# Context projections of layers 1 to 3 beside the first steps of layer 0's recurrence

## The chip, the cores and the metric

The kernel runs on one core of one Trainium2 chip. The metric is the device time of one execution in microseconds (us). The engines are named as in the profile: PE is TensorE (PEld its weight loads), DVE is VectorE, ACT is ScalarE, POOL is GpSimd, SP is SyncE, whose queue (SPq) issues most DMAs. L12 is line 12 of the kernel before, unless the text says that it is the changed kernel's.

## The reference, cut to what matters

Four layers work on tokens x (4 batches of 512 tokens, width 256) and a context (4 batches of 64 rows, width 256). Each layer adds an attention over the context and a feed-forward part, each behind a layer norm and a gate.

```python
# layer 0: an LSTM over the 512 tokens, attending to the context in each step;
# then one of 8 experts per token
x = x + tanh(g_xattn[0]) * _L0_xattn_ref(ctx_1024, _layernorm(x), ...)
x = x + tanh(g_ffn[0]) * _L0_ffn_ref(_layernorm(x), ...)
# layer 1: attention in both directions; two of 8 experts
x = x + tanh(g_xattn[1]) * _L1_xattn_ref(_layernorm(x), ctx_1024, ...)
    K_sub = _linear(subword_emb, Wk_s, bk_s)     # of the context alone
    V_sub = _linear(subword_emb, Wv_s, bv_s)
    Q_sub = _linear(subword_emb, Wq_s, bq_s)
...
# layer 2: additive attention; the experts that hold 0.8 of the probability
    txt_proj = einsum('btd,de->bte', textual_features, Ws)   # context alone
# layer 3: 16 heads of 64; then an int8 matmul
    k = (context @ Wk.T).reshape(b, nk, H, DH)   # context alone
    v = (context @ Wv.T).reshape(b, nk, H, DH)
```

The six lines marked or named by the context (K_sub, V_sub, Q_sub, txt_proj, k, v) need nothing of x. All arithmetic is float32 but for the last matmul.

## The kernel before, in words

**Setup** (lstm, L245). SP loads the LSTM's weights, then the first two pairs of expert weights (two calls of fetch, four DMAs of 1 MB) into a ring of three slots, each with a place for an up and a down matrix, 1 MB each. The transposed context, ctxT, stays for the whole kernel.

**Recurrence** (L360). The 512 steps of layer 0 are a serial chain, one lstm_step each: h times two weights on PE (L816, L825), the attention's tanh on ACT (L834), scores on PE (L843), softmax, attended features into the gates (L867), transpose of the gates (L875, DVE), gate arithmetic, and the new h (hb, L893, DVE). Each instruction of a step is pinned to the program's order on its engine. Work that is not on the chain is put in a planner, Later (L162): tasks with an engine, a cost, and the tasks that they wait for. At fixed places of each step, fill emits as many as fit a budget: on PE one after whh's matmuls, two after the scores and two after the gates' (SLOT_A, SLOT_B, SLOT_C), on DVE one between alb (L863) and the transpose of the gates (L875). A task goes out only when what it needs on another engine was emitted one step earlier for DVE and ACT, four for SP. Before step 64 the planner holds the projections of the gates for later tokens (every 32 steps); after each block of 64 steps (TB), block_tasks adds the experts of layer 0 for that block. The planner's accumulators "up" have two buffers. An expert matrix is fetched (L111, the DMAs are L122 and L125) when the last matmul of the one before in its place is done. After the last step the planner is drained.

Instructions that are not pinned are placed by a scheduler: if an instruction's tile is free early in the program, it may land among the recurrence's.

**Tail.** Layer 1 starts with norm (xn, L988) and its loads (load_l1, L1497: wqc, wks, wvs, wqs, wkc, wvc, wg, b, interp, in this order on SP). context_l1 (L1515) first makes hbg from b, then 4 projections for ksT and qsT (two matmuls each, 128x256) and 4 for vs. load_l2 (L1649) and context_l2 (L1665) do the same for layer 2: wslide from its vector l_vec (L1672), txtT (two projections), rep (L1682), and off from the mask (L1690 to L1692). All matmuls of the tail stand in program order on PE, and are listed under the helper's line L936.

The experts of layers 1 and 2 are run in two halves of two batches each: b0 and b1 (layer 1), c0 and c1 (layer 2). weave (L906) takes one piece of the main generator, an expert's pieces, and then side pieces at a given ratio; part_of ends the side part after a number of pieces. back (L1461) is such a side part: it gathers expert rows for 128 tokens with an indirect DMA issued by POOL (yg, L1477, 8 buffers) and adds each to the tokens on DVE (L1469), the add standing more than three pairs behind. Beside c1 run the backs of batches 0 and 1 and the start of layer 3: load_l3 (L1782: wk, wv, wq, wo, bo, rhs), context_l3 (L1800: kT, 8 projections evicted by DVE, L1812; v, 4 of width 512 evicted by ACT), then heads and the int8 matmul. The backs of batches 2 and 3 follow c1.

Of the kernel before, what the change touches and what calls it, by code (L numbers as in the profile page):

```python
# [21 lines left out]
FP = mybir.dt.float32  # L22
# [222 lines left out]
def lstm(net):  # L245
    tc, nc, a = net.tc, net.nc, net.a
    with ExitStack() as st:
# [19 lines left out]
        with tc.tile_pool(name="l_set", bufs=1) as pool, tc.tile_pool(  # L267
# [21 lines left out]
            nc.sync.dma_start(w1b, a["L0_whh1"])  # L289
            net.fetch()  # L290
            net.fetch()

# [68 lines left out]
def recurrence(net, w, pools):  # L361
# [21 lines left out]
    h = w["h0"]  # L383
    for t in range(S):
        i, u = divmod(t, P)
        if u == 0 and i + 1 < TPB:
            norm_x(net, later, w, pools, xb, i + 1)
        v = t % TB
        if v == 0:
            n = t // TB  # L390

            assert n < 3 or all(x["at"] for x in used[n - 3])
            hb = two.tile([P, 2, TB, NB], FP, name="hb", bufs=3)
            cb = two.tile([P, 2, TB, NB], FP, name="cb", bufs=3)
        if t % 32 == 0 and t and t // 32 + 1 < NJ:
            gates_of_block(net, later, w, pools, xb, ge, t // 32 + 1)
        lstm_step(net, pools["step"], ps, w, later, ge, t, h, hb[:, :, v], cb[:, :, v], ga[t % 2], ga[1 - t % 2])
        h = hb[:, :, v]
        if t > TB and t % 8 == 4:
            net.fill()  # L400
        if v == TB - 1:
            used.append(block_tasks(net, later, w, moe0, pools, n, hb, cb))
    later.drain()


# [1055 lines left out]
def back(t, pool, kind, batches, group, got):  # L1461
# [9 lines left out]
    for b in batches:  # L1471
        for i in range(TPB):
            for k in range(0, kind.most, 2):
                here = []
                for kk in (k, k + 1):
                    y = pool.tile([P, D], FP, name="yg", bufs=8)
                    nc.gpsimd.indirect_dma_start(  # L1477
                        out=y[:, :], out_offset=None, in_=got["res"][:, :],
                        in_offset=bass.IndirectOffsetOnAxis(
                            ap=got["index"][:, b - group[0], kk, i : i + 1], axis=0  # L1480
                        ),
                    )
                    c = got["cw"][:, b - group[0], kk, i : i + 1]
                    here.append((y, net.xtok[:, b * TPB + i, :], c))
                due.append(here)
                if len(due) > 3:
                    add()
                yield
# [8 lines left out]
def load_l1(net, pool):  # L1497
    nc, a = net.nc, net.a
    w = {}
    for n in ("wqc", "wks", "wvs", "wqs", "wkc", "wvc"):  # L1500
        w[n] = pool.tile([P, KD, D], FP, name=f"l1_{n}")
        nc.sync.dma_start(w[n], a[f"L1_{n}"])
    w["wg"] = pool.tile([P, 2 * KD, D], FP, name="l1_wg")
    nc.sync.dma_start(w["wg"], a["L1_wg"])
    w["b"] = pool.tile([P, 7, 2], FP, name="l1_b")
    nc.sync.dma_start(w["b"], a["L1_b"])
    w["interp"] = pool.tile([SC, S], FP, name="l1_interp")
# [6 lines left out]

def context_l1(t, w, pool):  # L1515

    net = t.net
    nc = t.nc

    w["hbg"] = pool.tile([P, 2], FP, name="hbg")  # L1520
    nc.vector.tensor_scalar_mul(w["hbg"], w["b"][:, 6, :], 0.5)
    for n in ("ks", "qs"):
        w[f"{n}T"] = pool.tile([P, 2, NB * SC], FP, name=f"{n}T")
        for oc in range(2):
            ps = t.ps(P, NB * SC)
            mm(nc, ps, ((w[f"w{n}"][:, k, ts(oc, P)], net.ctxT[:, k, :]) for k in range(KD)))
            nc.vector.tensor_scalar_add(w[f"{n}T"][:, oc, :], ps, w["b"][:, BIAS[n], oc : oc + 1])
    w["vs"] = pool.tile([SC, NB, D], FP, name="vs")
    for b in range(NB):
        ps = t.ps(SC, D)  # L1530
        mm(nc, ps, ((net.ctxT[:, k, ts(b, SC)], w["wvs"][:, k, :]) for k in range(KD)))
        nc.vector.tensor_copy(w["vs"][:, b, :], ps)

# [115 lines left out]
def load_l2(net, pool):  # L1649
    nc, a = net.nc, net.a  # L1650
    w = {}
    for n in ("ws", "w"):
        w[n] = pool.tile([P, KD, D], FP, name=f"l2_{n}", tag="rt" if n == "ws" else "l2_w")
        nc.sync.dma_start(w[n], a[f"L2_{n}"])
    w["vec"] = pool.tile([P, 4, KD], FP, name="l2_vec")
    nc.sync.dma_start(w["vec"], a["L2_vec"])
    w["bc"] = pool.tile([P, 2], FP, name="l2_bc")
# [6 lines left out]

def context_l2(t, w, pool):  # L1665

    net = t.net
# [4 lines left out]
    nc.vector.tensor_copy(w["wslide"][:, :, 31], w["vec"][:, 0, :])  # L1672
    w["txtT"] = pool.tile([P, KD, NB * SC], FP, name="txtT")
    for ec in range(KD):
        ps = t.ps(P, NB * SC)
        mm(nc, ps, ((w["ws"][:, k, ts(ec, P)], net.ctxT[:, k, :]) for k in range(KD)))
        nc.vector.tensor_scalar_add(w["txtT"][:, ec, :], ps, w["vec"][:, 1, ec : ec + 1])
        yield
    w["cw"] = pool.tile([P, 2, NB * SC], FP, name="cw")
# [102 lines left out]
def load_l3(net, pool):  # L1782
    nc, a = net.nc, net.a
    w = {}
    w["wq"] = pool.tile([P, KD, 1024], FP, name="l3_wq")

    wkv = pool.tile([P, 2, KD, 1024], FP, name="l3_wkv", tag="atT")
    w["wk"], w["wv"] = wkv[:, 0], wkv[:, 1]
    for n in ("wk", "wv", "wq"):
        nc.sync.dma_start(w[n], a[f"L3_{n}"])  # L1790
    w["wo"] = pool.tile([P, NP, D], FP, name="l3_wo")
# [7 lines left out]

def context_l3(t, w, pool):  # L1800

# [3 lines left out]
    nc.vector.memset(w["ones"], 1.0)  # L1805
    w["kT"] = pool.tile([P, NP, NB * SC], FP, name="kT")

    w["v"] = pool.tile([P, NB, NP, 64], FP, name="v")
    for pr in range(NP):
        ps = t.ps(P, NB * SC)  # L1810
        mm(nc, ps, ((w["wk"][:, k, ts(pr, P)], net.ctxT[:, k, :]) for k in range(KD)))
        nc.vector.tensor_copy(w["kT"][:, pr, :], ps)  # L1812
        yield
    for b in range(NB):
        ps = t.ps(P, 512)
        for par in range(2):
            mm(nc, ps[ts(par, 64), :], (
                (net.ctxT[:, k, ts(b, SC)], w["wv"][:, k, ts(par, 512)]) for k in range(KD)
            ))
        nc.scalar.copy(w["v"][:, b].rearrange("p n d -> p (n d)"), ps)  # L1820
        yield

# [169 lines left out]
def gated_blocks_kernel(ctx: ExitStack, tc: tile.TileContext, a, out):  # L1992
# [5 lines left out]
    for layer, kind in KINDS.items():  # L1998
        for g, x in enumerate(got[layer]):
            x["rows"] = net.scratch(f"rows{layer}{g}", kind.rows, kind.end)  # L2000
            x["res"] = net.scratch(f"res{layer}{g}", kind.end, kind.end)
    lstm(net)
    t = Tail(net, ctx)
# [3 lines left out]
    t.b1 = mp.tile([P, 3, F_MOE[2] // P], FP, name="b1_in")  # L2007
    with ExitStack() as right, ExitStack() as work:

# [7 lines left out]
        with tc.tile_pool(name="attn1", bufs=1) as p1:  # L2017
            w1 = load_l1(net, p1)
            w2 = load_l2(net, p2)
            context_l1(t, w1, p1)  # L2020
            pk = Picks(t, sort)
# [19 lines left out]
            run(behind(1, l1, 0))  # L2041
            weave(b0.sure(), chain(behind(1, l1, 2), context_l2(t, w2, p2)), 1.1)
            b0.rest()
# [15 lines left out]
    def layer3(b, over=False):  # L2059
        return chain(heads(t, w3, p3, b, over), quantised(t, w3, p3, b, out))  # L2060

    start = chain(
        back_of(2, 0, [0]), turns(context_l3(t, w3, p3), back_of(2, 0, [1])), layer3(0), layer3(1)
    )
    weave(c1.sure(), part_of(start, 105), 0.8)
    c1.rest()
# [116 lines left out]
```

## Time and profile before

| what | value |
|---|---|
| median of three timed runs | 5496.51 us (5494.62 to 5498.4) |
| profiled execution | 5493.01 us, of which its span is 5491.3 |
| mean granted PE clock | 0.954 |
| PE busy | 4605.5 us (84%) |
| DVE busy | 2441.6 us (44%) |
| ACT busy | 2532.1 us (46%) |
| POOL busy | 466.3 us (8%) |
| recurrence, first to last h | 54.26 to 3463.69 us |

The page of the profile lists busy times, the span in 40 slices, DMA queues, the chain that ended last, and the costliest groups of instructions. The timeline of an engine has one row per instruction or run of equal instructions: start, duration, engine, line, operation, tiles and shapes, and in brackets how long the engine stood idle before and what ended that. The windows give the engines' busy times and the granted clock of a stretch. A float32 matmul appears as two passes, so two matmuls are four rows of PE.

### The profile page before, as it was taken

How to read it: one execution, taken by the hardware profiler on the slowest of the kernel's cores; microseconds unless marked ns; L12 is line 12 of the kernel's file. 1: busy time of each engine (PE TensorE's matmuls, PEld its weight loads, DVE VectorE, ACT ScalarE, POOL GpSimd, SP SyncE). 2: the span in 40 equal slices, each digit the busy share in tenths (PEclk: the TensorE clock that was granted, in tenths of full speed). 3: DMA queues.
4: the chain of work that ended last, by engine and by line, in shares of the span. 5: the costliest groups of instructions: out<-in, count | busy, mean ns of one | idle time of the engine just before them, and what ended most of it. 6: DMA issues, size and time to landing. Idle time of an engine off the chain costs nothing. (4 is left out here: it accounts for less than half of the span.)

```text
span 5491.3 us, 139195 instructions
## 1 busy us (share of the span) xinstructions
PE 4605.5 (84%) x57504; PEld 2504.8 (46%) x57504; DVE 2441.6 (44%) x9780; ACT 2532.1 (46%) x7118; POOL 466.3 (8%) x884
## 2 busy tenths in 40 slices
PE   5566699789999899999999989987978598869967
PEld 2222244334444344444444434754533365757744
DVE  3545555555555555555555555224422342121145
ACT  2233365556656566566556555412266265213212
POOL 1000100000100100000000000001111201230030
PEclk8999999999999999999999999988999799989978
DMA  5000022122212122122122111313543333543210
GB/s 191 2 2 2 2 78 109 40 74 94 93 67 102 54 90 94 61 75 97 68 81 102 71 42 49 118 40 130 194 140 126 136 117 120 191 158 136 94 53 8
DMA packets 117963, 480.46 MB, mean 87 GB/s; under 512 B 23473, under 2 KB 62786, under 8 KB 87938
## 3 DMA queue, kind: packets, MB, share of 16 engines
q1 hardware_dynamic: 105026, 437.85, 22.3%
q0 software_dynamic: 12288, 33.57, 1.9%
q8 instruction: 455, 7.45, 0.6%
q14 instruction: 194, 1.59, 0.1%
HBM read 434.65 MB, written 137.89 MB: 104 GB/s over the span
## 5 line engine op out<-in xcount | busy, mean ns | idle before, releaser
L867 PE MATMUL psf<-fw,alb 128*4 128x256 f32 x8192 | 540.7, 381 | 171.4 <-DVE alb L863 141.0
L720 PE MATMUL ps_up<-xm,ring 128*128 128x256 f32 x2048 | 614.8, 412 | 3.4 <-ACT h L730 3.3
L751 PE MATMUL ps_down<-ring,h 128*128 128x256 f32 x2048 | 580.5, 399 | 0.0
L825 PE MATMUL psf<-whh,hb 128*4 128x256 f32 x8176 | 542.4, 383 | 0.0
L720 PEld LDWEIGHTS ps_up<-xm,ring 128*128 128x128 f32 x2048 | 335.9, 188 | 226.7 <-issue 174.2
L855 ACT ACTIVATE al<-psr,stat 128x64 f32<-128x64 f32 x1024 | 312.4, 309 | 272.6 <-DVE stat L854 272.0
L751 PEld LDWEIGHTS ps_down<-ring,h 128*128 128x128 f32 x2048 | 356.9, 189 | 156.9 <-issue 111.6
L834 ACT ACTIVATE e<-e 128x256 f32<-128x256 f32 x512 | 213.4, 417 | 466.4 <-DVE e L833 465.3
L854 DVE TENSOR_REDUCE stat<-psr 128x1 f32<-128x64 f32 x1024 | 229.5, 225 | 419.7 <-PE psr L843 409.2
L833 DVE TENSOR_TENSOR e<-fproj,hw 128x256 f32<-128x256 f32 x1024 | 395.4, 427 | 17.6
L816 PE MATMUL psa<-wh,hb 128*4 128x64 f32 x8176 | 209.7, 220 | 228.1 <-DVE hb L893 226.6
L843 PE MATMUL psr<-e,vrep 128*32 128x64 f32 x16384 | 349.8, 224 | 47.1 <-ACT e L834 41.8
L474 PE MATMUL psf<-ge,ident 128*4 128x256 f32 x4096 | 319.7, 384 | 65.2 <-DVE gt L875 65.1
L894 POOL COPY cb<-ga 128x8 f32<-128x8 f32 x512 | 97.0, 189 | 3234.2 <-DVE ga L886 3234.2
L843 PEld LDWEIGHTS psr<-e,vrep 128*32 128x32 f32 x16384 | 262.5, 109 | 236.2 <-ACT e L834 228.4
L936 PE MATMUL ps_up<-xT,ring 128*128 128x256 f32 x1280 | 309.5, 393 | 72.2 <-ACT h L1425 52.3
L1717 ACT ACTIVATE h<-featT,txtT 128x512 f32<-128x512 f32 x512 | 324.7, 710 | 97.5 <-PE psr L936 64.1
L878 ACT ACTIVATE ga<-gt 128x32 f32<-128x32 f32 x512 | 116.8, 228 | 541.9 <-DVE gt L875 541.7
L875 DVE STREAM_TRANSPOSE gt<-psf 128x256 f32<-128x256 f32 x512 | 230.3, 450 | 302.7 <-PE psf L867 302.2
L867 PEld LDWEIGHTS psf<-fw,alb 128*4 128x4 f32 x8192 | 117.0, 84 | 518.2 <-DVE alb L863 517.7
L816 PEld LDWEIGHTS psa<-wh,hb 128*4 128x4 f32 x8176 | 114.5, 86 | 487.2 <-DVE hb L893 487.2
L936 PEld LDWEIGHTS ps_up<-xT,ring 128*128 128x128 f32 x1280 | 244.4, 195 | 150.0 <-ACT h L1425 55.7
(418 smaller groups left out, 6565.7 us busy)
## 6 DMA issues: line engine op xcount, KB each, us to landing
ring<-in_L_w_dram SPq DMA_DIRECT2D x208, 1024.0 KB
ring<-in_L_w_dram SPq DMA_DIRECT2D x120, 512.0 KB
res<-y SPq DMA_DIRECT2D x120, 128.0 KB
rows_in<-rows SPq DMA_DIRECT2D x40, 256.0 KB
rows_in<-rows SPq DMA_DIRECT2D x40, 128.0 KB
rows<-in_x_dram SPq DMA_DIRECT2D x2, 1920.0 KB
res<-in_x_dram SPq DMA_DIRECT2D x2, 1920.0 KB
xtok<-in_x_dram SPq DMA_DIRECT2D x4, 512.0 KB
```

What stands on the lines that cost most here:

```text
L474: net.tc.keep_in_program_order(net.nc.tensor.matmul(out[32 * q : 32 * q + NB, :], lhsT=sel, rhs=ge[t // 32][:, ts(q, 256)], start=True, st ...
L720: yield nc.tensor.matmul(cell["ps"][:, f % 2, :], lhsT=ex["w"][:, k, ts(f, P)], rhs=box["x"][:, k, :], start=k == 0, stop=k == KD - 1,)
L751: yield nc.tensor.matmul(cell["ps"], lhsT=ex["h"][:, f, ts(p, P)], rhs=ex["down"][:, f, :], start=f == 0, stop=f == 7,)
L816: pin(nc.tensor.matmul(ps["a"][32 * q : 32 * q + NB, :], lhsT=h[:, c, :], rhs=w["wh"][:, c, ts(q, 64)], start=c == 0, stop=c == 1,))
L825: pin(nc.tensor.matmul(psf[32 * q : 32 * q + NB, :], lhsT=h[:, c, :], rhs=w["whh"][:, c, ts(q, 256)], start=False, stop=False,))
L833: pin(nc.vector.tensor_add(e[:, p], w["fproj"][:, p], bc(hw[:, :, ts(p, 2)], 3, SC)))
L843: pin(nc.tensor.matmul(ps["r"][p][ts(2 * b + i, 32), :], lhsT=w["vrep"][:, c, :], rhs=ev[:, ::-1, :] if i else ev, start=c == 0, stop=c == ...
L855: pin(nc.scalar.activation(al[:, p], ps["r"][p], AF.Exp, bias=stat[:, p, 0:1], accum_out=stat[:, p, 1:2]))
L867: pin(nc.tensor.matmul(psf[32 * q : 32 * q + NB, :], lhsT=alb[:, p], rhs=w["fw"][:, p, ts(q, 256)], start=False, stop=p == 1,))
L875: pin(nc.vector.transpose(gt.rearrange("p g b -> p (g b)"), psf))
L936: return lambda *a, **k: self.tc.keep_in_program_order(fn(*a, **k))
L1717: nc.scalar.activation(h, featT[:, ec, :], AF.Tanh, bias=w["txtT"][:, ec, col : col + 1])
```

## The change

The projections that need only the context and weights move to the start of the kernel. load_context loads their weights and the vectors of layers 1 and 2 in the setup, where the experts' first fetches stood; the four small matrices share one place of the ring, wk and wv take one place each. context_tasks gives the planner 26 jobs at step 4, one accumulator each: 4 for ksT and qsT, 4 for vs, 2 for txtT, 8 for kT (two matmuls each) and 8 for v (four matmuls each, of width 256 in place of 512); all are evicted by DVE. The experts' four fetches are emitted at step 60. The results lie in new pools on the right side of the memory, allocated ahead of the recurrence (16 KB per partition for kT and v, some 10 KB for the rest), and the pools that were on the right start behind them. The gathers' buffers go from 8 to 6, the adds stand more than two pairs behind, and the side pieces beside c1 go from 105 to 93, at a ratio of 0.7 for 0.8. What is left of context_l1, context_l2 and context_l3 is renamed.

```diff
--- before.py
+++ after.py
@@ -287,8 +287,7 @@
             nc.sync.dma_start(small[:, 28:36], a["L0_bhh1"])
             nc.sync.dma_start(w1, a["L0_wih1"])
             nc.sync.dma_start(w1b, a["L0_whh1"])
-            net.fetch()
-            net.fetch()
+            load_context(net)
@@ -382,6 +381,12 @@
     gates_of_x(net, ps["f"], ge, 0)
     h = w["h0"]
     for t in range(S):
+        if t == 4:
+            context_tasks(net, later, pools["up"])
+        if t == TB - 4:
+            assert not later.left()
+            net.fetch()
+            net.fetch()
@@ -401,6 +406,84 @@
     later.drain()
+
+
+def load_context(net):
+
+    nc, a, c = net.nc, net.a, net.of_context
+    r = net.ring
+    for i, n in enumerate(("L1_wks", "L1_wqs", "L1_wvs", "L2_ws")):
+        c[n] = r[:, 0, 0, ts(i, 512)].rearrange("p (k d) -> p k d", k=KD)
+    for i, n in enumerate(("L3_wk", "L3_wv")):
+        c[n] = r[:, i, 1 - i].rearrange("p (k d) -> p k d", k=KD)
+    nc.sync.dma_start(c["b"], a["L1_b"])
+    nc.sync.dma_start(c["vec"], a["L2_vec"])
+    for n in ("L1_wks", "L1_wqs", "L1_wvs", "L2_ws", "L3_wk", "L3_wv"):
+        nc.sync.dma_start(c[n], a[n])
+
+
+def context_tasks(net, later, up):
+
+    nc, c, ctxT = net.nc, net.of_context, net.ctxT
+    v = nc.vector
+
+    def job(shape, parts, out, cost=1.0, after=()):
+        box, head = {}, None
+        for of, lhsT, rhs, k in parts:
+
+            def part(of=of, lhsT=lhsT, rhs=rhs, k=k):
+                if not box:
+                    box["ps"] = up.tile(shape, FP, name="ps_cx", tag="up")
+                yield nc.tensor.matmul(
+                    of(box["ps"]), lhsT=lhsT, rhs=rhs, start=k == 0, stop=k == KD - 1
+                )
+
+            last = later.add("PE", part, after, cost, takes=[] if head else ["up"])
+            head = head or last
+        later.add("DVE", lambda: [out(box["ps"])], [last], frees=[("up", head)])
+
+    def all_of(x):
+        return x
+
+    n = NB * SC
+    for name in ("ks", "qs"):
+        for oc in range(2):
+            job(
+                [P, n], [(all_of, c[f"L1_w{name}"][:, k, ts(oc, P)], ctxT[:, k, :], k) for k in range(KD)],
+                lambda ps, name=name, oc=oc: v.tensor_scalar_add(
+                    c[f"{name}T"][:, oc, :], ps, c["b"][:, BIAS[name], oc : oc + 1]
+                ),
+            )
+    for b in range(NB):
+        job(
+            [SC, D], [(all_of, ctxT[:, k, ts(b, SC)], c["L1_wvs"][:, k, :], k) for k in range(KD)],
+            lambda ps, b=b: v.tensor_copy(c["vs"][:, b, :], ps),
+        )
+    for ec in range(KD):
+        job(
+            [P, n], [(all_of, c["L2_ws"][:, k, ts(ec, P)], ctxT[:, k, :], k) for k in range(KD)],
+            lambda ps, ec=ec: v.tensor_scalar_add(c["txtT"][:, ec, :], ps, c["vec"][:, 1, ec : ec + 1]),
+        )
+    for pr in range(NP):
+        job(
+            [P, n], [(all_of, c["L3_wk"][:, k, ts(pr, P)], ctxT[:, k, :], k) for k in range(KD)],
+            lambda ps, pr=pr: v.tensor_copy(c["kT"][:, pr, :], ps),
+        )
+
+    for b in range(NB):
+        for h in range(2):
+            job(
+                [P, 256], [
+                    (
+                        lambda ps, par=par: ps[ts(par, 64), :], ctxT[:, k, ts(b, SC)],
+                        c["L3_wv"][:, k, ds(512 * par + 256 * h, 256)], k,
+                    )
+                    for par in range(2) for k in range(KD)
+                ],
+                lambda ps, b=b, h=h: v.tensor_copy(
+                    c["v"][:, b, ts(h, 4)].rearrange("p n d -> p (n d)"), ps
+                ),
+            )
@@ -1473,7 +1556,7 @@
             for k in range(0, kind.most, 2):
                 here = []
                 for kk in (k, k + 1):
-                    y = pool.tile([P, D], FP, name="yg", bufs=8)
+                    y = pool.tile([P, D], FP, name="yg", bufs=6)
@@ -1483,7 +1566,7 @@
...
                 due.append(here)
-                if len(due) > 3:
+                if len(due) > 2:
@@ -1497,13 +1580,13 @@
 def load_l1(net, pool):
     nc, a = net.nc, net.a
     w = {}
-    for n in ("wqc", "wks", "wvs", "wqs", "wkc", "wvc"):
+    for n in ("wqc", "wkc", "wvc"):
         w[n] = pool.tile([P, KD, D], FP, name=f"l1_{n}")
         nc.sync.dma_start(w[n], a[f"L1_{n}"])
     w["wg"] = pool.tile([P, 2 * KD, D], FP, name="l1_wg")
     nc.sync.dma_start(w["wg"], a["L1_wg"])
-    w["b"] = pool.tile([P, 7, 2], FP, name="l1_b")
-    nc.sync.dma_start(w["b"], a["L1_b"])
+    for n in ("b", "ksT", "qsT", "vs"):
+        w[n] = net.of_context[n]
@@ -1512,24 +1595,10 @@
 BIAS = {n: i for i, n in enumerate(("qc", "ks", "vs", "qs", "kc", "vc", "g"))}
 
 
-def context_l1(t, w, pool):
-
-    net = t.net
-    nc = t.nc
+def gate_bias(t, w, pool):
 
     w["hbg"] = pool.tile([P, 2], FP, name="hbg")
-    nc.vector.tensor_scalar_mul(w["hbg"], w["b"][:, 6, :], 0.5)
...
+    t.nc.vector.tensor_scalar_mul(w["hbg"], w["b"][:, 6, :], 0.5)
@@ -1649,11 +1718,10 @@
 def load_l2(net, pool):
     nc, a = net.nc, net.a
     w = {}
-    for n in ("ws", "w"):
-        w[n] = pool.tile([P, KD, D], FP, name=f"l2_{n}", tag="rt" if n == "ws" else "l2_w")
-        nc.sync.dma_start(w[n], a[f"L2_{n}"])
-    w["vec"] = pool.tile([P, 4, KD], FP, name="l2_vec")
-    nc.sync.dma_start(w["vec"], a["L2_vec"])
+    w["w"] = pool.tile([P, KD, D], FP, name="l2_w")
+    nc.sync.dma_start(w["w"], a["L2_w"])
+    for n in ("vec", "txtT"):
+        w[n] = net.of_context[n]
@@ -1662,20 +1730,13 @@
-def context_l2(t, w, pool):
-
+def constants_l2(t, w, pool):
     net = t.net
     nc = t.nc
 
     w["wslide"] = pool.tile([P, KD, 63], FP, name="wslide")
     nc.vector.memset(w["wslide"], 0.0)
     nc.vector.tensor_copy(w["wslide"][:, :, 31], w["vec"][:, 0, :])
...
@@ -1783,11 +1844,9 @@
     nc, a = net.nc, net.a
     w = {}
     w["wq"] = pool.tile([P, KD, 1024], FP, name="l3_wq")
-
-    wkv = pool.tile([P, 2, KD, 1024], FP, name="l3_wkv", tag="atT")
-    w["wk"], w["wv"] = wkv[:, 0], wkv[:, 1]
-    for n in ("wk", "wv", "wq"):
-        nc.sync.dma_start(w[n], a[f"L3_{n}"])
+    nc.sync.dma_start(w["wq"], a["L3_wq"])
+    for n in ("kT", "v"):
+        w[n] = net.of_context[n]
@@ -1797,28 +1856,12 @@
-def context_l3(t, w, pool):
+def constants_l3(t, w, pool):
 
     net = t.net
     nc = t.nc
     w["ones"] = pool.tile([1, P], FP, name="ones")
     nc.vector.memset(w["ones"], 1.0)
...
@@ -1999,13 +2042,24 @@
+
+    late = ctx.enter_context(tc.tile_pool(name="late", bufs=1, side="right"))
+    right = ExitStack()
+    early = right.enter_context(tc.tile_pool(name="early", bufs=1, side="right"))
+    net.of_context = {
+        name: pool.tile(shape, FP, name=f"cx_{name}") for name, pool, shape in (
+            ("b", early, [P, 7, 2]), ("vec", early, [P, 4, KD]), ("ksT", early, [P, 2, NB * SC]),
+            ("qsT", early, [P, 2, NB * SC]), ("vs", early, [SC, NB, D]),
+            ("txtT", early, [P, KD, NB * SC]), ("kT", late, [P, NP, NB * SC]), ("v", late, [P, NB, NP, 64]),
+        )
+    }
     lstm(net)
...
-    with ExitStack() as right, ExitStack() as work:
+    with right, ExitStack() as work:
@@ -2017,7 +2071,7 @@
         with tc.tile_pool(name="attn1", bufs=1) as p1:
             w1 = load_l1(net, p1)
             w2 = load_l2(net, p2)
-            context_l1(t, w1, p1)
+            gate_bias(t, w1, p1)
@@ -2039,7 +2093,7 @@
             b1 = Blocks(t, KINDS[1], first, got[1][1], KINDS[1].sure % 3)
             b0 = Blocks(t, KINDS[1], first, got[1][0], 0, b1)
             run(behind(1, l1, 0))
-            weave(b0.sure(), chain(behind(1, l1, 2), context_l2(t, w2, p2)), 1.1)
+            weave(b0.sure(), chain(behind(1, l1, 2), constants_l2(t, w2, p2)), 1.1)
@@ -2060,9 +2114,9 @@
     start = chain(
-        back_of(2, 0, [0]), turns(context_l3(t, w3, p3), back_of(2, 0, [1])), layer3(0), layer3(1)
+        back_of(2, 0, [0]), turns(constants_l3(t, w3, p3), back_of(2, 0, [1])), layer3(0), layer3(1)
     )
-    weave(c1.sure(), part_of(start, 105), 0.8)
+    weave(c1.sure(), part_of(start, 93), 0.7)
```

More of the change, by code (lines that the diff above doesn't have):

```diff
@@ L1512 @@
 BIAS = {n: i for i, n in enumerate(("qc", "ks", "vs", "qs", "kc", "vc", "g"))}
-def context_l1(t, w, pool):
-    net = t.net
-    nc = t.nc
+def gate_bias(t, w, pool):
     w["hbg"] = pool.tile([P, 2], FP, name="hbg")
[L1521 to L1532, printed above, removed]
+    t.nc.vector.tensor_scalar_mul(w["hbg"], w["b"][:, 6, :], 0.5)
 def both_ways(t, w, pool, b):
@@ L1672, in context_l2 @@
     nc.vector.tensor_copy(w["wslide"][:, :, 31], w["vec"][:, 0, :])
[L1673 to L1678, printed above, removed]
     w["cw"] = pool.tile([P, 2, NB * SC], FP, name="cw")
@@ L1805, in context_l3 @@
     nc.vector.memset(w["ones"], 1.0)
[L1806 to L1821, printed above, removed]
     w["identb"] = pool.tile([P, P], BF, name="identb")
```

## Prediction

> **What bounds the kernel now.** I read the page's forty slices first, then the DVE and SP timelines of the first slices, then the windows of the stages that the change touches, then the PE groups and the POOL timeline of the last layers.
>
> ```profile
> PE   5566699789999899999999989987978598869967
> PEclk8999999999999999999999999988999799989978
> ```
>
> A slice is 137 us. Slices 0 to 24 are the recurrence of layer 0, a serial chain of 512 steps; the rest are experts' matmuls, with dips of PE and of its clock where layers meet. No one engine bounds the whole, so each moved piece must be priced in its own stage.
>
> The update of h (DVE, L893) ends each step. Between steps 5 and 40 it comes every 6.50 us. In steps 2 to 4 it does not:
>
> ```profile
> 60.48 0.17 DVE L893 SCALAR_TENSOR_TENSOR hb<-ga,tcn 128x8 f32<-128x8 f32 x1 [0.28 <-ACT tcn L888]
> 79.87 0.17 DVE L1672 COPY wslide<-l_vec 128x2 f32<-128x2 f32 x1 [15.48 <-DMA l_vec<-in_L_vec_dram]
> 83.85 0.17 DVE L893 SCALAR_TENSOR_TENSOR hb<-ga,tcn 128x8 f32<-128x8 f32 x1 [0.34 <-ACT tcn L888]
> 92.54 0.17 DVE L893 SCALAR_TENSOR_TENSOR hb<-ga,tcn 128x8 f32<-128x8 f32 x1 [0.33 <-ACT tcn L888]
> 100.38 0.17 DVE L893 SCALAR_TENSOR_TENSOR hb<-ga,tcn 128x8 f32<-128x8 f32 x1 [0.33 <-ACT tcn L888]
> ```
>
> The differences are 23.37, 8.69 and 7.84. DVE stands 15.48 us before a constant of layer 2 that the scheduler put among step 2's instructions, since its tile was free from the start. Its DMA is late because SP was held:
>
> ```profile
> 43.91 17.05 SPq L513 DMA_DIRECT2D xh<-in_x_dram  x4
> 74.46 0.33 SPq L1656 DMA_DIRECT2D l_vec<-in_L_vec_dram  x1
> ```
>
> The three other stages, from the windows (columns: stretch, its length, busy time and count of each engine, granted clock, DMA share, GB/s):
>
> ```profile
> core 0: us, PE busy (x) PEld busy (x) DVE busy (x) ACT busy (x) POOL busy (x), PEclk, DMA share, GB/s
> 54.00:101.00 47.00, 22.49 (x382) 8.46 (x382) 14.45 (x67) 8.85 (x40) 5.64 (x9) 0.65 0.52 174
> 3627.00:3648.00 21.00, 14.19 (x45) 9.27 (x46) 4.99 (x14) 0.40 (x1) 0.00 (x0) 0.62 0.33 107
> 4900.00:4960.00 60.00, 60.00 (x282) 47.26 (x281) 5.31 (x10) 16.36 (x39) 0.00 (x0) 1.00 0.44 152
> ```
>
> The second is layer 1's start, a chain on a slow clock. The third is a stretch of layer 2's second half (c1) in which PE is full: work taken from PE there comes off the end.
>
> **The change part by part**, against the profiled execution, 5493.0 us (span 5491.3 and 1.7 around it). The median of the three timed runs is 3.5 us above it; I add that at the end.
>
> *Early steps.* In the changed program's order, layer 2's DVE constants stand behind the last step: the new pools on the right push layer 2's pool onto memory that the recurrence uses. The layer's vector is loaded with the first transfers, and no other DVE instruction of the early steps waits for a DMA. So the excess goes: 16.9 + 2.2 + 1.3 = **-20.4**. Next late is the step's own chain, 6.50.
>
> *The added jobs.* From step 4, one per step: 26 jobs, 68 matmuls and 26 evictions. An eviction (0.42 us for a copy, 0.48 with a bias, by the rows of kT and ksT) stands on DVE ahead of this row, whose idle covers it:
>
> ```profile
> 59.08 0.45 DVE L875 STREAM_TRANSPOSE gt<-psf 128x256 f32<-128x256 f32 x1 [0.74 <-PE psf L867]
> ```
>
> Behind it on DVE is the gate chain of the step. Two matmuls (four 128x256 passes at 0.216 us) go into a step, four for a v job. Later steps that already carry expert matmuls show 6.58 against 6.50, so 26 x 0.08 = **+2.1**. From both sides: 0, and 0.28 per step (the 6.78 of steps with gates' work), +7.3. SP issues nine transfers at the start instead of four, five more at 0.45, 2.3 us; behind them are tables and rows that only the first experts' tasks need, after step 64, which hide it. The experts' four fetches move to step 60 and wait there for the jobs' matmuls, which ended by step 30; one is hoisted to the start. 4 MB at 174 GB/s is 24 us, under the four steps (26 us) to the first possible use; without that cover, up to 24.
>
> *Layer 1's start.*
>
> ```profile
> 3624.41 1.38 DVE L988 TENSOR_SCALAR xn<-xtok,ln_mv,ln_rstd 128x256 f32<-128x256 f32 x4
> 3636.52 0.17 DVE L1521 TENSOR_SCALAR hbg<-l_b 128x2 f32<-128x2 f32 x1 [10.72 <-DMA l_wg<-in_L_wg_dram]
> ```
>
> ```profile
> 3630.40 3.75 PE L936 MATMUL ps_side<-ctxT,l_wks 128*128 128x256 f32 x8 [6.63 <-DMA l_wks<-in_L_wks_dram]
> 3637.12 3.78 PE L936 MATMUL ps_side<-ctxT,l_wqs 128*128 128x256 f32 x8 [2.98 <-DVE ksT L1527]
> 3645.56 0.49 PE L936 MATMUL ps_side<-upper,ones 128*128 128x128 f32 x2
> 3647.87 2.41 PE L936 MATMUL ps_side<-xT,l_wqc 128*128 128x512 f32 x5 [0.34 <-DVE xT L1003]
> ```
>
> The normalised tokens are ready at 3625.8, the projections of the context stand in front, and wqc's matmuls start at 3647.87. Without them wqc decides, issued at 3626.99; wks landed 3.0 us after its issue, so about 3630.4: -17.5. But the clock: wks' passes run at half speed for some 10 us, and now the token projections meet that. From both sides 0 and 5 us (half of 10); I take 3, since steady matmuls replace a broken chain: **-14.5** (-12.5 to -17.5). The Trainium skill's page "TensorE: Matmul & The Clock Gate", Part 1, has the clock doubled after about 3.4 us of sustained matmuls; by that the loss is half of 3.4, an estimate of 1.7, and the sum would be 1.3 lower. The trace's slow passes last longer, with waits between them, so it does not decide that.
>
> *Layer 2's start.* Two txtT jobs leave a PE-bound stage: 8 passes of 0.216, **-1.7** (0 to -2.7).
>
> *c1.*
>
> ```profile
> L936 PE MATMUL ps_side<-ctxT,l_wkv 128*128 128x256 f32 x32 | 8.2, 379 | 0.0
> L936 PE MATMUL ps_side<-l_wkv,ctxT 128*64 128x512 f32 x32 | 7.8, 605 | 0.0
> ```
>
> The 32 passes for kT start 0.216 apart: 6.9. The v passes start in pairs 14 ns apart, each job from 4934.51 to 4936.38, with 0.2 lost at its ends: four jobs, 8.2. **-15.1** (0 to -16).
>
> *Fewer gather buffers.* Issue to the end of the add is 3.2 to 7.3 us where DVE is prompt; six buffers at 1.25 us each cover 7.5. Where DVE is held, POOL stops two gathers sooner, as it already does here:
>
> ```profile
> 5261.16 0.95 POOL L1477 DMA_INDIRECT yg<-res,g_index  x1 [4.26 <-DVE xtok L1469]
> ```
>
> Two gathers are 2.5 us, and the tail's 48 gathers lie on the chain that ends last: **+2.5** (0 to +8, three such stops). Behind the stopped gather on POOL are only gathers; the adds wait for them. The page "DMA: Bandwidth & Descriptors" of the Trainium skill, "Anatomy of one DMA", gives about 2.0 us plus the bytes for a GpSimd DMA; by it (2.3 us, an estimate) six buffers would never be short and the term 0. The 3.2 to 7.3 here are longer.
>
> *Moved constants.* Four DMAs of layer 2 now stand on SP after the last step, ahead of a ring fetch (4 x 0.4 us); the mask's conversion then holds DVE some 3 us with an add of experts' output behind it, where DVE shows 2 to 13 us idle before each add and PE has its next expert: 0 to +3. The sorter's constants and the gate bias go to layer 1's start. Together **+1**.
>
> Sum: -20.4 + 2.1 - 14.5 - 1.7 - 15.1 + 2.5 + 1 = -46.1; 5493.0 becomes 5446.9, on the median's scale **5450.4**.
>
> **Rivals**, on that scale.
> *The early stall finds another cause* (a job's matmul waits in PE's queue for its weights). For: SP's 17 us hold stays. Against: those weights are issued before it, where ring fetches stood. 5450 + 20 = 5471.
> *c1 does not shorten*, since transfers or the gathers set its end. For: PE idles 39.76 us there. Against: 60.00 of 60 and 0.44 DMA share. 5466.
> *Slower: the gathers collide with more expert transfers.* In before, one store of expert rows sat behind three 1 MB fetches while 48 gathers shared the DMA engines, and PE stood:
>
> ```profile
> 4868.91 3.48 PE L936 MATMUL ps_up<-xT,ring 128*128 128x256 f32 x8 [39.76 <-ACT h L1425]
> ```
>
> With 0.7 side pieces per expert piece and no kT and v between, the second batch's gathers fall beside other fetches. Each repeat costs 39.8; the gain of 46 is gone, and 11 more, from 57 us of new PE idle, so two repeats: 5530. Against: the tail's 48 gathers show none.
> *The collision falls away instead*: 5411.
> *The jobs hide nothing*: 18 jobs' 72 passes and 32 paired v passes at half speed (0.43) are 45, evictions 12, in all 57 instead of 2.1: 5505. Against: the 6.58 row.
>
> **How the numbers follow.** A measurement here tells about 0.2% (11 us) from no change. Forecast (5436 to 5464) 0.56; early stall 0.12; c1 0.13; collisions 0.06; collision gone 0.08; jobs on the path 0.05. The first three hold 0.81, and with their bounds reach 5430 to 5480. Faster 0.89, same 0.05, slower 0.06.
>
> **What would show it.** h every 6.5 to 6.8 us from step 2; no DVE wait for layer 2's vector; wqc's matmuls some 5 us after the last xn; c1 shorter by 15 us, no l_wkv groups; POOL stops of 5 to 7 us in the tail. It is wrong if early steps stay above 8 us, PE idles over 40 us at the gathers, or c1's fetches stall PE.

## The result, and the profile after

The changed kernel took **5438.10 us** (median of four runs, 5436.06 to 5438.90) beside 5495.57 for the kernel before on the same chip: 57.5 us less, ratio 0.9894 with a 95% interval of 0.9877 to 0.9912. The forecast was 5450.4, from 5430 to 5480. The profiled execution has a span of 5437.2 us, 54.1 less.

The slices of the page after, PE busy and PE's granted clock in tenths:

```profile
PE   6756698889999899999999989987988599879967
PEclk9999999999999999999999999988998699889978
```

The first slice's clock is 9 for 8, and its PE 6 for 5. The DVE timeline of the first steps (start, duration, and in brackets the idle time before and its releaser):

```profile
60.06 0.17 DVE L976 SCALAR_TENSOR_TENSOR hb<-ga,tcn 128x8 f32<-128x8 f32 x1 [0.28 <-ACT tcn L971]
66.56 0.17 DVE L976 SCALAR_TENSOR_TENSOR hb<-ga,tcn 128x8 f32<-128x8 f32 x1 [0.33 <-ACT tcn L971]
73.37 0.17 DVE L976 SCALAR_TENSOR_TENSOR hb<-ga,tcn 128x8 f32<-128x8 f32 x1 [0.34 <-ACT tcn L971]
77.45 0.48 DVE L453 TENSOR_SCALAR cx_ksT<-ps_cx,cx_b 128x256 f32<-128x256 f32 x1
78.28 0.45 DVE L958 STREAM_TRANSPOSE gt<-psf 128x256 f32<-128x256 f32 x1 [0.35 <-PE psf L950]
79.88 0.17 DVE L976 SCALAR_TENSOR_TENSOR hb<-ga,tcn 128x8 f32<-128x8 f32 x1 [0.34 <-ACT tcn L971]
```

Steps of 6.50, 6.81 and 6.51 us stand where 23.37, 8.69 and 7.84 stood. The last one holds the first job: its eviction of 0.48 us takes DVE's idle time before the gates' transpose from 0.74 to 0.35, and the step is no longer for it. The windows of the three stages, in the order of those shown of before:

```profile
core 0: us, PE busy (x) PEld busy (x) DVE busy (x) ACT busy (x) POOL busy (x), PEclk, DMA share, GB/s
54.00:101.00 47.00, 33.68 (x681) 14.39 (x678) 25.45 (x113) 14.79 (x67) 6.01 (x11) 1.00 0.41 146
3606.00:3627.00 21.00, 18.43 (x64) 11.40 (x64) 4.38 (x14) 5.04 (x7) 0.50 (x2) 0.84 0.24 76
4850.00:4910.00 60.00, 60.00 (x287) 52.09 (x287) 3.46 (x5) 18.09 (x44) 0.00 (x0) 1.00 0.55 195
```

The early clock is 1.00 for 0.65, and c1 is as full as before, with the experts' rows and the first of layer 3's queries, none of kT and v. Layer 1's start, on DVE, SP and PE:

```profile
3605.02 1.38 DVE L1071 TENSOR_SCALAR xn<-xtok,ln_mv,ln_rstd 128x256 f32<-128x256 f32 x4
3607.66 0.17 DVE L1601 TENSOR_SCALAR hbg<-cx_b 128x2 f32<-128x2 f32 x1 [1.26 <-DMA xtok<-xh]
```

```profile
3607.63 0.33 SPq L1585 DMA_DIRECT2D l_wqc<-in_L_wqc_dram  x1
```

```profile
3608.42 0.80 PE L1019 MATMUL ps_side<-upper,ones 128*128 128x128 f32 x2 [4.04 <-POOL upper L1181]
3609.60 1.97 PE L1019 MATMUL ps_side<-ident,xn 128*128 128x128 f32 x8
3611.50 4.96 PE L1019 MATMUL ps_side<-xT,l_wqc 128*128 128x512 f32 x8
3616.30 3.60 PE L1019 MATMUL ps_side<-xT,l_wkc 128*128 128x512 f32 x8
```

wqc's matmuls start 5.1 us after the last xn ends (3606.4), where they started 22.1 after it. wqc's eight passes take 4.96 us, wkc's eight behind them 3.60: a slow clock, from the first of these rows on, that is over within wqc's passes. In before wqc's passes had the full clock from the start:

```profile
3647.87 3.70 PE L936 MATMUL ps_side<-xT,l_wqc 128*128 128x512 f32 x8 [0.34 <-DVE xT L1003]
```

Two stops that the forecast named are still there, the PE's at c1's first gathers, shorter, and POOL's in the tail:

```profile
4817.86 3.78 PE L1019 MATMUL ps_up<-xT,ring 128*128 128x256 f32 x8 [26.33 <-ACT h L1508]
```

```profile
5205.57 1.07 POOL L1560 DMA_INDIRECT yg<-res,g_index  x1 [5.06 <-DVE xtok L1552]
```

### The profile page after: what moved, and what is told of

It is laid out like the page before. It is cut to its first block, busy times and chain, and to the rows that moved or that the text cites. A ratio compares the mean times of both kernels' runs of the same rounds, so it can differ in the third digit from the quotient of the medians.

```text
span 5437.2 us, 139292 instructions
## 1 busy us (share of the span) xinstructions
PE 4618.9 (85%) x57536; PEld 2505.2 (46%) x57536; DVE 2444.1 (45%) x9788; ACT 2531.7 (47%) x7114; POOL 467.7 (9%) x884
## 3 DMA queue, kind: packets, MB, share of 16 engines
q1 hardware_dynamic: 105026, 437.85, 22.5%
## 5 line engine op out<-in xcount | busy, mean ns | idle before, releaser
L916 DVE TENSOR_TENSOR e<-fproj,hw 128x256 f32<-128x256 f32 x1024 | 395.4, 427 | 17.6
L1778 ACT ACTIVATE h<-featT,cx_txtT 128x512 f32<-128x512 f32 x512 | 324.0, 710 | 99.4 <-PE psr L1019 61.2
L926 PEld LDWEIGHTS psr<-e,vrep 128*32 128x32 f32 x16384 | 260.1, 109 | 223.8 <-ACT e L917 216.4
```

What stands on the lines that cost most here:

```text
L916: pin(nc.vector.tensor_add(e[:, p], w["fproj"][:, p], bc(hw[:, :, ts(p, 2)], 3, SC)))
L926: pin(nc.tensor.matmul(ps["r"][p][ts(2 * b + i, 32), :], lhsT=w["vrep"][:, c, :], rhs=ev[:, ::-1, :] if i else ev, start=c == 0, stop=c == ...
L1778: nc.scalar.activation(h, featT[:, ec, :], AF.Tanh, bias=w["txtT"][:, ec, col : col + 1])
```

## The experiments

Twelve runs in three sets; the kernels of a set share a chip and the runs of the kernel before. That kernel took 5415.6 us in the first set, 5494.5 in the second and 5414.1 in the third; the chips of the first and third set are called quick below, that of the second and that of the first comparison slow. So only times of one set are subtracted, and stages are compared between chips only where the text says so. All ratios below are to the kernel before of the set.

### First set

**b_vec**, before with two loads moved:

```diff
+            nc.sync.dma_start(net.l2_vec, a["L2_vec"])
+            nc.sync.dma_start(net.l2_mask, a["mask"].partition_broadcast(P))
             net.fetch()
             net.fetch()
```

(the tiles lie in the pool that stays; load_l2 uses them).

> Before, with one edit: layer 2's vector and mask are loaded with the setup's DMAs, so that the DVE constants that the scheduler puts into step 2 find their data. Theory (a constant that waits for its DMA holds DVE and with it the recurrence): steps 2 to 4 last 6.5 to 7 us each and the time falls by 18 to 20 us, to about 5476. Rival (another late transfer or SP's 17 us hold takes its place): a step above 10 us stays among the first five and the time falls by less than 10 us.

5393.54, 22.0 us less, 0.9955 (0.9938 to 0.9972). Its DVE timeline:

```profile
60.47 0.17 DVE L897 SCALAR_TENSOR_TENSOR hb<-ga,tcn 128x8 f32<-128x8 f32 x1 [0.27 <-ACT tcn L892]
66.97 0.17 DVE L897 SCALAR_TENSOR_TENSOR hb<-ga,tcn 128x8 f32<-128x8 f32 x1 [0.33 <-ACT tcn L892]
73.78 0.17 DVE L897 SCALAR_TENSOR_TENSOR hb<-ga,tcn 128x8 f32<-128x8 f32 x1 [0.34 <-ACT tcn L892]
```

The stall is gone without a single job moved; the scheduler now has the copy of wslide at 32.9 us, ahead of the recurrence. The fifth h ends at 80.5 us, near the changed kernel's 80.0, so the step forecast at -20.4 is shown alone, and it needs two small DMAs and no more. Whether one of the two would do was not tried.

**b_yg6**, before with six gather buffers:

```diff
-                    y = pool.tile([P, D], FP, name="yg", bufs=8)
+                    y = pool.tile([P, D], FP, name="yg", bufs=6)
...
-                if len(due) > 3:
+                if len(due) > 2:
```

> Before, with the gathers' buffers at 6 and the adds more than two pairs behind, nothing else. Theory A (in the changed kernel the longest PE stall at c1's first 48 gathers fell from 39.8 to 26.3 us because six buffers slow the gathers, 67.9 us for 60.5, and so leave the DMA engines to the expert transfers in front of a store): the stall falls by 8 to 14 us here too, the gathers take over 65 us, and the time is 5483 to 5490. Theory B (it fell since wk and wv, 2 MB, are no longer loaded and kT and v no longer stand between the gathers): the stall stays within 3 us of 39.8 and the time within 4 us of 5495.6.

5402.38, ratio 0.9975 (0.9965 to 0.9984), 13 us less. That looks like theory A, and is not: on this chip c1's first 48 gathers take 60.5 us with six buffers and 59.8 with eight (b_vec), and the PE idle beside them is 25.6 against 28.0. The gain is in the tail: from the first of its gathers to the end 239.2 us against b_vec's 252.7. What makes it is taken up in the third set, since the edit does more than change a count.

**a_yg8**, the changed kernel with eight buffers for layer 2: every fourth pair of gathers takes its tiles from layer 3's pool (p3, given as more), and the adds stand more than three pairs behind.

```diff
-                    y = pool.tile([P, D], FP, name="yg", bufs=6)
+                    if more and n % 8 >= 6:
+                        y = more.tile([P, D], FP, name="yh", bufs=2)
+                    else:
+                        y = pool.tile([P, D], FP, name="yg", bufs=6)
+                    n += 1
...
-                if len(due) > 2:
+                if len(due) > (3 if more else 2):
```

> The changed kernel, with eight gather buffers for layer 2's expert rows (the two more in layer 3's pool) and the adds more than three pairs behind, as before. Theory A (six buffers shorten the stall at the first 48 gathers): the gathers take about 60 us, the stall goes back to 36 to 42 us and the time rises by 8 to 13 us to 5446 to 5451. Theory B (the absent loads and projections do it): the stall stays near 26 us; the time is 5436 to 5440, or 1 to 3 us lower if the tail's gathers gain.

5367.17, 0.9904 (0.9888 to 0.9921). Its idle PE at the gathers is 27.9 us in all, beside 26.4 in a_kv_in_c1 and 25.6 in b_yg6 with six. The changed kernel was not run on this chip; the third set has the pair.

**a_kv_in_c1**, the changed kernel with context_l3's loops put back:

```diff
-    for pr in range(NP):
+    for pr in range(0):
...
+        mm(nc, ps, ((w["wk"][:, k, ts(pr, P)], net.ctxT[:, k, :]) for k in range(KD)))
...
-    weave(c1.sure(), part_of(start, 93), 0.7)
+    weave(c1.sure(), part_of(start, 105), 0.8)
```

> The changed kernel, with kT and v computed in c1 again as before (wk and wv loaded there, 105 side pieces at 0.8); the early jobs without those 16, and their weights still loaded at the start though nothing reads them. Six gather buffers. The forecast's term (15.1 us of PE work): 5453, with the stall at the gathers still near 26 us under theory A. Under theory B the stall goes back to some 40 us as well: 5463 to 5468. If c1 were not bound by PE there: within 4 us of 5438.

5364.52, 0.9900 (0.9884 to 0.9917), 51.1 us below before; the changed kernel is 59.7 below it in the third set, so kT and v are worth about 8.6, on chips that are alike but not the same one. By stages: c1 from its first gather to the tail's is 413.5 us here and 400.7 in a_third, 12.8 more, and the tail 243.0 against 242.1. So c1 shows 12.8 of the 15.1 us at which the PE work was put, and the medians less.

### Second set

**b_again** and **a_again**, the two kernels unchanged.

> The kernel before, unchanged, for a profile on the chip on which the other kernels of this set run (the earlier set ran on a chip where it takes 5416 us and not 5496). If that chip differs in its transfers alone, the recurrence ends within 3 us of 3463.7, and the difference lies in the stages that fetch experts, the PE stall of 39.8 us at c1's gathers among them.

> The changed kernel, unchanged. If its gain is the sum of stages that do not hang on transfers (20 early steps, 16 layer 1's start, 15 kT and v), it is 46 to 54 us on any chip. If the shorter stall at c1's gathers is part of it (13 us on the first chip), it is 38 to 45 us where that stall is short, under 12 us in before.

Before: 5494.52 (nine runs); a_again 5440.60, 53.9 less, 0.9903 (0.9888 to 0.9919). This chip is like the one of the first comparison, and 53.9 lies within the 46 to 54 that was expected without the shorter stall; a chip with a short stall comes in the third set. Between this chip's and the first set's, the recurrence ends alike (3464.4 us in b_again, 3463.0 in b_yg6), and the difference lies in the experts' stages, as expected. Windows of c0 (layer 2's first half), first b_again, then b_vec, columns as above:

```profile
4335.00:4802.00 467.00, 412.01 (x2010) 285.42 (x2011) 137.43 (x427) 214.06 (x369) 62.99 (x65) 0.92 0.42 147
```

```profile
4293.00:4725.00 432.00, 398.60 (x2010) 281.03 (x2011) 137.52 (x427) 213.80 (x369) 63.14 (x65) 0.96 0.45 159
```

The same 2010 rows of PE take 35 us more there, with 55 us of idle PE for 33 and fewer GB/s. The stall at c1's gathers, in b_again, a_again and, on the quick chip, b_vec:

```profile
4871.01 3.58 PE L936 MATMUL ps_up<-xT,ring 128*128 128x256 f32 x8 [38.36 <-ACT h L1425]
```

```profile
4820.30 3.78 PE L1019 MATMUL ps_up<-xT,ring 128*128 128x256 f32 x8 [28.72 <-issue]
```

```profile
4763.32 3.78 PE L940 MATMUL ps_up<-xT,ring 128*128 128x256 f32 x8 [9.58 <-ACT h L1429]
```

**a_l1_back**, the changed kernel with the eight jobs for ksT, qsT and vs at layer 1's start again (b stays loaded at the start).

```diff
-    for n in ("wqc", "wkc", "wvc"):
+    for n in ("wqc", "wks", "wvs", "wqs", "wkc", "wvc"):
...
+    for n in ("ks", "qs"):
+        for oc in range(2):
+            ps = t.ps(P, NB * SC)
+            mm(nc, ps, ((w[f"w{n}"][:, k, ts(oc, P)], net.ctxT[:, k, :]) for k in range(KD)))
```

> The changed kernel, with ksT, qsT and vs computed at layer 1's start again, their weights loaded there (and still loaded at the start, where nothing reads them). Forecast's term: 14.5 us slower than the changed kernel (12.5 to 17.5), of which the first token projection starts 17 us later and 2 come back from the clock. Rival (the start is bound by its loads, not by the projections): under 5 us slower.

5447.15 (5440.88 to 5455.85), 0.9914 (0.9900 to 0.9927): 6.6 us above a_again, with runs that overlap. Its profile shows the stage:

```profile
3612.85 3.75 PE L1019 MATMUL ps_side<-ctxT,l_wks 128*128 128x256 f32 x8 [6.85 <-DMA l_wks<-in_L_wks_dram]
3616.39 2.10 PE L1019 MATMUL ps_side<-ctxT,l_wqs 128*128 128x256 f32 x8
3618.43 3.67 PE L1019 MATMUL ps_side<-l_wvs,ctxT 128*64 128x256 f32 x16
3624.34 3.70 PE L1019 MATMUL ps_side<-xT,l_wqc 128*128 128x512 f32 x8 [0.35 <-DVE xT L1086]
```

The median thus lies between the forecast's 12.5 to 17.5 and the rival's 5, and bears out neither. From the fourth xn's start to wqc's first matmul the profile has 16.7 us, against 5.5 in a_again and 22.5 and 18.9 in the two profiles of before. So in this profile the projections and the wait for their weights cost 11 us, not 15 to 17. In before, hbg, which reads b, stood on DVE until the load of wg, issued just ahead of b's, had landed, and the evictions of ksT stood behind it: PE waited 2.98 us for ksT in one profile and 2.12 in the other, and not here, where b is loaded early. That is all of the difference in the second profile (2.1 us). In the first the rest, 2.8 of 5.8, is qs' and vs' passes on a slower clock (3.78 and 4.79 us for 2.10 and 3.67). Moving b's load alone might bring the wait; it was not tried.

**a_twice**, the jobs done twice:

```diff
-        if t == 4:
+        if t in (4, 33):
             context_tasks(net, later, pools["up"])
```

> The changed kernel, with the 26 early jobs done a second time from step 33 on. Forecast's term (0.08 us a step): 1 to 3 us slower, steps 33 to 60 at 6.5 to 6.8. Rival (the jobs lie on the step's path): 26 steps longer by 0.5 us or more, over 13 us slower.

5438.79, 0.9899 (0.9884 to 0.9914), not told apart from a_again. The 26 steps with the first jobs take 170.3 us in both profiles, against 169.0 in b_again: 1.3 us for 26 jobs. The steps with the second ones stand at 6.53 to 6.59, but for three at 6.78, 6.81 and 6.88, of which two are at 6.78 without them. Steps 31 to 64 take 223.8 us with the second jobs, and without them 223.2 in a_again and 222.1 in the first profile after. The difference between these two is a slow stretch around step 43 (7.32 and 7.06 in a_again), which both profiles of before show, and of the changed kernel's some and others not; it does not tell of the jobs. Against 222.1 the second 26 jobs cost 1.7 us.

### Third set

> The changed kernel, unchanged, on the chip of this set, as the base of the next three. Where before takes some 5495 us: 5436 to 5444. Where it takes some 5416 us: 5354 to 5362 (with kT and v back in c1 it took 5364.5 there, and that part is worth 2 to 11 us if the stall at the gathers is short).

> The changed kernel with eight gather buffers and adds more than three pairs behind, for layer 2. Theory A (six buffers spread c1's first gathers over 68 us and spare c1 some 10 us of stall): where before takes 5495 us, gathers back to 60 to 62 us, stalls beside them back to 48 to 50 us in sum, and 8 to 12 us slower than the changed kernel. Theory C (that stall is only exchanged: the side pieces that c1 takes on make up for it): stalls as under A, the time within 4 us. Where before takes 5416 us: 8 to 12 us slower through the tail, if the adds' earlier place is what shortened it there.

> The changed kernel with eight gather buffers, but the adds more than two pairs behind as in the changed kernel. If the place of the adds in DVE's order decides, it is within 3 us of the changed kernel; if the number of buffers does, it is within 3 us of the kernel with eight buffers and three pairs.

> The changed kernel with c1's side part as before: 105 pieces at 0.8 in place of 93 at 0.7. The twelve more pieces are heads of layer 3. If c1 and the tail exchange work one for one, within 3 us of the changed kernel; if the tail is bound by its gathers and the pieces would have been hidden there, 5 to 15 us slower; if the tail's PE is the bound, up to 5 us faster.

**a_third**, the changed kernel: 5354.46, 59.7 less than before, 0.9884 (0.9869 to 0.9899). That is more than either range expected of a_again (46 to 54, or 38 to 45 on such a chip). **a_yg8_b**: 5367.04, 0.9909 (0.9896 to 0.9923), 12.6 above it. c1's gathers and stalls do not differ (59.5 us and 27.1 of idle PE against 59.8 and 25.2): theory A has nothing to stand on here, C neither. The difference is the tail, 251.4 us for 242.1. The POOL timelines of the tail, of a_third its only wait longer than 0.31 us, which is the one ahead of the first gather, and of a_yg8_b the longest of its waits for the adds:

```profile
5113.54 0.94 POOL L1560 DMA_INDIRECT yg<-res,g_index  x1 [339.96 <-DVE at L1928]
```

```profile
5140.11 0.95 POOL L1565 DMA_INDIRECT yg<-res,g_index  x1 [0.95 <-DVE xtok L1553]
```

a_yg8_b has four such stops (0.74, 0.45, 0.95 and 0.35 us), 2.5 us in all; its 48 gathers take 64.0 us for 60.1, and the other 5.4 of the tail's 9.3 come after the last gather. **a_yg8_d2**, eight buffers and two pairs (`len(due) > 2` in a_yg8), has 5361.10 (5355.58 to 5371.16), between the two, and neither side of its expectation holds. In its profile the tail is 245.0, 6.4 below a_yg8_b's, and c1 403.8, 2.8 above it.

What the two edits do apart is less plain than it looks, for the pair distance moves a third thing. With the adds more than two pairs behind, each back ends one piece sooner, and since part_of gives c1 a fixed number of pieces, two more pieces of layer 3's heads stand beside c1 and leave the tail. The rows show it: in a_yg8_b the tail holds 224 passes of the scores (kT with qT), in a_third and a_yg8_d2 192, and c1 has the 34 rows more (1769 for 1735); in b_yg6 the tail has 21 rows fewer than in b_vec. At the rate of a_r08, below (94 rows and 18.8 us less tail), 34 rows would be some 7 us of the tail, an estimate. So the 6.4 us are the adds' place and the moved pieces together. Over c1 and tail together a_third has 642.8 us, a_yg8_d2 648.8 and a_yg8_b 652.4: so counted, 6.0 go with the buffers and 3.6 with the pair distance. The times spread too far to settle the shares, and why eight buffers should be slower than six is open. **a_r08**, the changed kernel with part_of(start, 105) at 0.8: 5351.67 (5349.78 to 5353.73), 0.9882 (0.9867 to 0.9897), 2.8 below a_third with runs that overlap. c1 is 14.9 us longer and the tail 18.8 shorter in its profile: nearly one for one.

## Why the prediction was right, and where its terms were off

The stages, in us, from landmarks of the traces; before and after are the means of two profiles each, on like chips (before and b_again; after and a_again):

| stage, up to | before | after | measured | forecast |
|---|---|---|---|---|
| fifth h (steps 1 to 4) | 100.3 | 80.2 | -20.1 | -20.4 |
| last h | 3363.7 | 3365.3 | +1.6 | +2.1 |
| fourth xn of layer 1 (drain) | 161.7 | 161.7 | 0.0 | +1 with the sorter's constants |
| wqc's first matmul | 20.7 | 5.5 | -15.2 | -17.5 |
| c1's first gather | 1155.1 | 1151.8 | -3.3 | +3 clock, -1.7 txtT |
| tail's first gather (c1) | 432.1 | 414.5 | -17.6 | -15.1 |
| end (tail) | 257.0 | 259.2 | +2.2 | +2.5 |
| sum | 5490.7 | 5438.3 | -52.4 | -46.1 |

The sum is 6.3 us short of the profiles, and 11 short of the first pair of medians. The largest term is shown alone by b_vec; the rows from wqc on carry a spread. Between two profiles of the same stage c1 differs by up to 4.6 us, the tail by up to 4.9, the stretch from wqc to c1 by up to 5.2. With a_twice and a_l1_back, which are the changed kernel from wqc on, the means of four profiles after are -2.3 for that stretch, -16.6 for c1 and +0.5 for the tail. Terms of 2 us there agree with the forecast by luck or not at all.

**Early steps.** Right in cause and size; b_vec has the cause alone.

**Jobs.** Right: 1.3 us (1.7 for the second 26), and a_twice shows the rival, jobs on the step's path, wrong by a factor: it would have cost some 55 us.

**Moved constants.** They cost nothing that shows: the drain is 161.7 us in all profiles. DVE does stand 4.31 us before the mask's conversion after the last step, and the add behind it is not needed until later.

**Layer 1's start: the sum came out, its parts less well.** The rows of wqc and of the stretch behind it measure -18.5 together, and were forecast at -16.2; by pairs they are -16.4 (before to after) and -20.6 (b_again to a_again). The row of wqc is -17.0 in the first pair, as forecast, and -13.4 in the second: the working took 22.5 us and 10 us of half clock from one profile of before, where the granted clock was 0.62, and b_again has 18.9 us and 0.84 in the same 21 us. Of before's time, too, 2 to 3 us were the wait for ksT's eviction behind the loads of wg and b, and not the projections (a_l1_back). What the clock took back is smaller than 3 us. wqc's eight passes last 4.80 us to the start of wkc's, 1.26 more than before's 3.54, and from the sorter's first matmul to wqc's first it is 3.08 for 2.31: 2.0 us in all, and 2.4 in a_again. The Trainium skill's page "TensorE: Matmul & The Clock Gate", Part 1, has about 3.4 us of sustained matmuls to the full clock. Here the clock stays slow from 3608.42 to 3614.15, 5.7 us of nearly unbroken matmuls (wqc's first three passes take 0.78 to 1.02 us each, the others 0.43), and 6.5 us in a_again, so the loss lies between the page's estimate of 1.7 and the forecast's 3.

**c1: the size was about right, with something beside it.** The PE work alone was put at 15.1. The profiles give -19.9 (before to after) and -15.4 (b_again to a_again), and a_kv_in_c1 some 13 on the quick chips. Beside it two things run against each other on the slow chips: the idle PE at the gathers falls from 49.4 us to 39.4 (b_again to a_again), and c1 has two more side pieces, since the constants' generator yields 12 times less and each back once less while part_of gives up 12 (PE's rows in c1 go from 1803 to 1766, 37 fewer where 64 passes left). That the shorter stall comes from six buffers is not shown: on the quick chips the count changes neither the stall nor the gathers' pace. On the slow chip (60.5 and 62.3 us of gathers before, 67.9 and 67.8 after) it was not tried apart; buffers or the absent 2 MB of wk and wv stay open.

**Gathers: the size agrees by luck.** +2.5 against +2.2, where the tail's own spread is up to 4.9 us. On the slow chips the mechanism is there, since POOL's stop grows from 4.26 and 4.15 us to 5.06 and 5.62 (4.80 and 5.21 in a_l1_back and a_twice), but over four profiles the tail is only 0.5 longer. Where transfers are quicker the sign turns: the smaller setting gains 13.5 us of the tail in b_yg6 and 9.3 in a_third. The forecast priced the buffers, and neither the adds' place nor the two pieces that went from the tail to c1 with it; the shares are open. By the figure of the page "DMA: Bandwidth & Descriptors" of the Trainium skill, "Anatomy of one DMA", six buffers would never be short, an estimate. That agrees with a_third, where POOL never stops for an add in the tail, and not with the stops of 5 us on the slow chips. Those end on DVE, which in the first profile after stood 6.49 us idle before layer 3's maxima, with the adds behind them in its order.

**Rivals.** No second early stall, c1 did shorten, and the collision neither multiplied nor fell away: 49.4 and 49.8 us of idle PE in the two profiles of before became 36.9 to 40.6 in four of the changed kernel on such chips.

## What to carry to other kernels

An instruction without a pin goes where the scheduler finds its tile free, and then waits in the order of a serial chain: look in the first steps of a recurrence for idle time that ends on a DMA of a later stage; two small loads moved ahead were worth as much as the largest term of this change, and needed no job moved. Before pricing moved work by the stretch that it occupies, take out the waits that only share the stretch, as hbg's for b. A buffer count and the distance at which its consumer is placed are two edits, and where a generator's length sets how many pieces fit beside another stage, the distance is two edits by itself: count the rows of each stage before giving a stage's gain to one of them. A term smaller than the spread of its stage between profiles of one kernel is neither borne out nor refuted by one pair.

## What the runs showed of the hardware

The same kernel took 5495.6 and 5494.5 us on two chips, 5415.6 and 5414.1 on two others: 1.5%, more than the change. The recurrence of before is equal within 2 us (3464.4 and 3463.0); the stages that fetch experts are longer (c0 467 us for 432), and the stall at c1's gathers is 38.4 for 9.6. Kernels are to be compared on one chip. The granted clock over layer 1's start was 0.62 in one profile of the unchanged kernel and 0.84 in another.
